# Moving statistics, sums and skip products in a selective-scan kernel: where x's statistics run, where a late sum stands, and which skip products go together

## Chip, cores and metric

The kernel runs on one core of a Trainium2 chip. The metric is the device time of one execution in microseconds; before the change the median of 3 runs is 20936.09 us (20930.49 to 20946.7). All data are 32-bit floats.

## The reference

The input is x of shape (8, 384, 64, 64). Two layers follow each other, each as x + f(groupnorm(x)) with 32 groups. The first is attention over channels, the second a selective scan in four directions:

```python
x = x + L0(gn(x))                          # 1x1 convs, 3x3 depthwise convs, channel attention, projection
xs = cross_scan(gn(x))                     # k = 0 rows, 1 columns, 2 rows reversed, 3 columns reversed
dts, Bs, Cs = split(einsum('bkdl,kcd->bkcl', xs, x_proj_weight), (12, 16, 16))
dt = softplus(einsum('bkrl,kdr->bkdl', dts, dt_projs_weight) + dt_bias)
h = h * exp(dt * A) + dt * u * B           # along l, for each of 16 states n; u = xs
y = sum over n of h * C  +  Ds * u
x = x + gelu(layernorm(cross_merge(y)))
```

A has 4 x 384 x 16 entries, the sequence length is 4096.

## The kernel before

The outer loop goes over 8 images. For each, `channel_attention` runs first, then `selective_scan`. `load_x(b + 1)` fetches the next image near the end of the scan stage into the same three buffers of x, which come free one by one as their last reader, `weigh` of step 31, has run (periods 2, 4 and 6 of step 30). `x_stats` (line 154) takes statistics of the next image in 24 blocks of 128 x 512 on VectorE. The group norm at the start of the next attention stage needs all of them.

The scan stage is written as a hand-made software pipeline. A step s is one direction k and one chunk of 512 positions: 32 steps, 8 for each k. A step has 8 periods p, each of which handles two of the 16 states (a pair). `period(g)` with g = 8 s + p issues, in an order written by hand:

- on VectorE six scans of pair g (`step(0)` to `step(5)`, line 565: two states times three blocks of 128 channels);
- on ScalarE the decays exp(dt A) for scans two ahead (`next_decay(i)` makes the decay for scan i + 2, line 544; two PSUM buffers, so it waits until scan i has freed its own);
- on GpSimd the two products w B of pair g + 1 (`drive`, line 553), sometimes `weigh` for the next step;
- on TensorE, for pair o = g - 1, eight turns q (`turned(q)`, line 587: three transposes of h into one of two PSUM banks), each followed by `apply(q)`, which multiplies by C into `hc` on ScalarE (line 599) or, for the q in `on_dve`, on VectorE (line 601); then sums over the states of the pair into `py` (`add_up`, lines 622 and 628). The output of a step has 512 positions by 384 channels in four blocks `lb`; blocks 0 to 2 are summed in the period after the pair (`added(0..2)`), block 3 one period later (`add_up(o - 1, NJ)`), since its last apply (q = 7) runs only at the start of that period;
- on TensorE also the projections of step s + 2 (`projected(i)`, twelve pieces i over periods 2 to 7, line 451). For k = 1 and 3 these read x with a stride of 64 elements.

For k = 0 the skip connection sum(Ds) * x is added by twelve extra products per step (line 614, inside `add_up`, ahead of the sum of the same block).

Period 1 is the burst: it makes the step size of step s + 1 and adds the finished step s - 1 into `ys` (`take`).

Almost everything is wrapped in `pin`, which is `tc.keep_in_program_order`: the instruction stays behind the one written before it on its engine. What is not pinned is placed by the framework's scheduler. The statistics are not pinned, nor are the DMAs, which all go through SyncE's queue. The statistics are written after the last period: ten before the last `take`, fourteen after it.

What sets the order of the work around the change, in the period for p other than 1:

```python
turned(0); step(0); apply_c(o - 1, 7); turned(1)
if p >= 3: projected(2 * p - 4)
add_up(o - 1, NJ); next_decay(0); step(1); apply(0); turned(2)
next_decay(1); step(2); drive(g + 1, 1); apply(1); turned(3)
added(0); apply(2); turned(4); next_decay(2); step(3); apply(3); turned(5); added(1)
next_decay(3); step(4); apply(4); turned(6); apply(5); turned(7); added(2)
if p == 2: projected(0)
if p >= 2: projected(2 * p - 3)
next_decay(4); step(5); apply(6); next_decay(5)
```

Of the kernel before, what the change touches and what calls it, by code (L numbers as in the profile page):

```python
# [17 lines left out]
NJ = C // P  # L18
H = W = 64
L = H * W  # L20
CH = 512
NCH = L // CH
# [9 lines left out]
NP = N // 2  # L32
HP = P // 2
NQ = CH // HP
PX = 4

FT = 256
JUNK = 512
# [36 lines left out]
def tile_channel_attention_then_selective_scan(ctx: ExitStack, tc: tile.TileContext, a: dict):  # L75
    nc = tc.nc
# [66 lines left out]
    def load_x(b):  # L143

        xs = []
        for j in range(NJ):
            t = big.tile([P, L], F32, tag="x", bufs=NJ, name=f"x{b}_{j}")
            for h in range(2):
                nc.sync.dma_start(t[:, bass.ts(h, L // 2)], x_d[b, j, :, bass.ts(h, L // 2)])
            xs.append(t)  # L150
        stats = big.tile([P, NJ, NCH, nc.vector.BN_STATS_DIM], F32, tag="st0", name=f"st0{b}")
        return xs, stats

    def x_stats(x, stats, blocks):

        for j, c in blocks:
            nc.vector.bn_stats(stats[:, j, c, :], x[j][:, bass.ts(c, CH)])

    def channel_attention(b, x, stats, before):

# [217 lines left out]
    def selective_scan(b, x1, stats1):  # L378
# [10 lines left out]
        with ExitStack() as st:  # L389
# [18 lines left out]
            with tc.tile_pool(name=f"sn{b}", bufs=1) as np_:  # L408
# [4 lines left out]
                for c in range(NCH):  # L413
                    for j in range(NJ):
                        s = x1[j][:, bass.ts(c, CH)]
# [176 lines left out]
            def apply_c(g, q, eng):  # L592
                s, p = divmod(g, NP)
                if q % 2 == 0:
                    hcs[g, q // 2] = work.tile([P, 2, C], F32, tag="hc", bufs=6, name=f"hc{b}_{g}_{q}")
                out, src = hcs[g, q // 2][:, q % 2, :], pts.pop(q)[:, :C]
                scale = cts[s][:, p * NQ + q : p * NQ + q + 1]
                if eng is nc.scalar:
                    pin(eng.activation(out, src, AF.Copy, scale=scale))  # L599
                else:  # L600
                    pin(eng.tensor_scalar_mul(out, src, scale))  # L601

            def add_up(g, lb):

                s, p = divmod(g, NP)
                if p == 0 and lb == 0:
                    pys[s] = ps_y.tile([P, NJ, CH], F32, tag="py", name=f"py{b}_{s}")
                hc, py = hcs.pop((g, lb)), pys[s]
                k, c = steps[s][:2]

                if k == 0 and p >= 2 and p % 2 == lb % 2:
                    j = p // 2 - 1
                    o = py[:, lb, bass.ts(j, P)] if lb < NJ else py[:, j, C:]
                    pin(nc.tensor.matmul(
                        o, lhsT=x1[j][:, c * CH + lb * P : c * CH + (lb + 1) * P],
                        rhs=skip[:, j, :], start=False, stop=False,
                    ))

                flags = dict(start=p == 0 and lb < NJ, stop=p == NP - 1 and lb == NJ)
                if lb < NJ:  # L620
                    for f in range(2):
                        pin(nc.tensor.matmul(  # L622
                            py[f * HP : (f + 1) * HP, lb, :C], lhsT=pair, rhs=hc[:, f, :], **flags
                        ))
                else:
                    for j in range(NJ):
                        for f in range(2):
                            pin(nc.tensor.matmul(  # L628
                                py[f * HP : (f + 1) * HP, j, C:], lhsT=pair,
                                rhs=hc[:, f, bass.ts(j, P)], **flags,  # L630
                            ))
# [61 lines left out]
            def period(g):  # L693

                o, s, p = g - 1, g // NP, g % NP  # L700
                last = g == S * NP
                burst = p == 1 and s + 1 < S
                on_dve = {3, 4, 5} if burst else {0: {2}, 2: {4}}.get(p, set())
                taken = s - 1 if p == 1 and s > 0 else None

                def step(i):
                    if not last:
                        scan(g, *divmod(i, NJ))

                def next_decay(i, home=None):  # L710
                    if not last:
                        decay(g, *divmod(i + 2, NJ), home)

                def apply(q):
                    if o >= 0:
                        apply_c(o, q, nc.vector if q in on_dve else nc.scalar)

                def turned(q):
                    if o >= 0:
                        turn(o, q)  # L720

                def added(lb):
                    if o >= 0:
                        add_up(o, lb)

                def projected(i):
                    if s + 2 < S:
                        project(s + 2, i)

                def take_all():  # L730
                    if taken is not None:
                        for i in range(NJ):
                            take(taken, i)

                if not last:
                    h2s[g] = work.tile([P, NJ, CH, 2], F32, tag="h", bufs=3, name=f"h{b}_{g}")
                    if p == 2:
                        sum_of(s)
                if o >= 0:
                    keep_last(o)  # L740
                fetch(g + 3)
                drive(g + 1, 0)
                if p == 3 and s + 1 < S:
                    mingle_c(s + 1)
                if p in (2, 4, 6) and s + 1 < S:
                    weigh(s + 1, p // 2 - 1)
                turned(0)
                step(0)
                if o >= 1:
                    apply_c(o - 1, NQ - 1, nc.scalar)  # L750
                turned(1)
                if p >= 3:
                    projected(2 * p - 4)
                if o >= 1:
                    add_up(o - 1, NJ)
                next_decay(0)
                step(1)
                apply(0)
                turned(2)
                next_decay(1)  # L760
                step(2)
                drive(g + 1, 1)
                apply(1)
                if burst:
                    pds = step_matmuls(s + 1)
                    apply(2)
                    next_decay(2)
                    next_decay(3, work)
                    step_size(s + 1, pds)
                    step(3)  # L770
                    step(4)
                    take_all()
                    step(5)
                    turned(3)
                    turned(4)
                    added(0)
                    apply(3)
                    turned(5)
                    apply(4)
                    turned(6)  # L780
                    added(1)
                    next_decay(4)
                    next_decay(5)
                    apply(5)
                    turned(7)
                    added(2)
                    apply(6)
                    return
                turned(3)
                if p == 1:  # L790
                    take_all()
                added(0)
                if p == 0 and 0 < s < S - 1:
                    lay_out(s + 1)
                apply(2)
                turned(4)
                next_decay(2)
                step(3)
                apply(3)
                turned(5)  # L800
                added(1)
                next_decay(3)
                step(4)
                apply(4)
                turned(6)
                apply(5)
                turned(7)
                added(2)
                if p == 2:
                    projected(0)  # L810
                if p >= 2:
                    projected(2 * p - 3)
                if p == 0 and s < S:
                    turn_c(s)
                next_decay(4)
                step(5)
                apply(6)
                next_decay(5)
                if p == 0 and s < S:
                    keep_c(s)  # L820

            x_next = None
            for g in range(S * NP + 1):
                period(g)
                if g == (S - 1) * NP + 1 and b + 1 < B:
                    x_next = load_x(b + 1)
            apply_c(S * NP - 1, NQ - 1, nc.scalar)
            add_up(S * NP - 1, NJ)
            blocks = [(j, c) for j in range(NJ) for c in range(NCH)]
            if x_next:  # L830
                x_stats(*x_next, blocks[:10])
            for i in range(NJ):
                take(S - 1, i)
            if x_next:
                x_stats(*x_next, blocks[10:])
        return y_d, x_next

    def token_norm(b, keep, work, y_d):
# [110 lines left out]
```

## Time and profile before

| | us |
|---|---|
| median of 3 runs | 20936.09 |
| profiled execution | 20922.88 |
| its span | 20921.1 |
| scan stage of one image, first scan to end of the last (images 0 to 6 / 7) | 2109.0 to 2111.5 / 2091.2 |
| from the start of the last period of an image to the first scan of the next | 499.8 to 504.0 |

The scan stages are about four fifths of the span. Their structure is seen best in the length of each period, taken from the trace as the distance between the first scans of two periods (median over images and steps, us):

| steps | direction now / two steps ahead | p 0 | 1 | 2 | 3 | 4 | 5 | 6 | 7 |
|---|---|---|---|---|---|---|---|---|---|
| 0 to 5 | rows, with skip / rows | 7.71 | 11.00 | 8.30 | 7.58 | 7.60 | 8.27 | 7.55 | 8.26 |
| 6 and 7 | rows, with skip / columns | 7.73 | 10.99 | 8.31 | 7.95 | 7.89 | 8.46 | 7.89 | 8.46 |
| 8 to 13 | columns / columns | 7.71 | 10.83 | 8.30 | 7.95 | 7.75 | 7.75 | 7.75 | 7.76 |
| 14 and 15 | columns / rows | 7.71 | 10.83 | 8.30 | 7.43 | 7.55 | 7.55 | 7.55 | 7.55 |
| 16 to 21 | rows / rows | 7.71 | 10.83 | 8.24 | 7.44 | 7.49 | 7.49 | 7.49 | 7.49 |
| 22 to 29 | rows, columns / columns | 7.71 | 10.83 | 8.24 | 7.89 | 7.70 | 7.69 | 7.69 | 7.69 |
| 30 | columns / none | 7.71 | 10.83 | 9.40 | 10.01 | 11.17 | 10.01 | 11.20 | 10.01 |

The rows differ in the direction of the step itself, in whether the projections of two steps ahead are contiguous (rows) or strided (columns), and in whether the step carries skip products. In a row of the profile the columns are the line, the engine, the operation, output and inputs with shapes, and the count; after the bar stand the busy time, the mean duration in ns, and the idle time of the engine just ahead of them with what ended it. A timeline line gives start and length in us of a run of like instructions, and in brackets the idle time ahead of it.

### The profile page before, as it was taken

The numbers are of one execution on the slowest core, as the hardware profiler recorded it, in microseconds if no ns is written. First come the engines' busy times: TensorE is split into PE (matmuls) and PEld (weight loads), VectorE is DVE, ScalarE is ACT, GpSimd is POOL, SyncE is SP. The second block draws the span as 40 slices with busy tenths as digits, with TensorE's granted clock in tenths as the row PEclk, the third lists the DMA queues.
The fourth block names the chain that finished last, engine by engine and source line by source line (L and its number), as shares of the span: only waits on it lengthen the run. The fifth ranks groups of instructions, "written<-read, shape, count | busy, mean of one in ns | idle before, by whom it ended". The sixth has DMA issues, their size and how long they took to land. (4 is left out here: it accounts for less than half of the span.)

```text
span 20921.1 us, 319325 instructions
## 1 busy us (share of the span) xinstructions
PE 19277.1 (92%) x118256; PEld 10697.2 (51%) x118256; DVE 19312.5 (92%) x17310; ACT 18022.9 (86%) x32267; POOL 15437.3 (74%) x6918
## 2 busy tenths in 40 slices
PE   7999989999899998999989999899998999989998
PEld 4555445555455554555445555455544555445554
DVE  8999989999899988999889998899988999889998
ACT  3999949999599985999859998599985999859998
POOL 0999809998199981999719997199971999729997
PEclk8999989999899998999989999899998999989999
DMA  1222322223223232222322223223232232322223
GB/s 41 78 91 93 95 75 81 91 92 96 73 81 91 92 99 70 81 91 92 102 69 81 91 92 102 70 79 91 93 99 71 81 92 92 97 71 82 91 91 116
DMA packets 953163, 1807.95 MB, mean 86 GB/s; under 512 B 125904, under 2 KB 646352, under 8 KB 945456
## 3 DMA queue, kind: packets, MB, share of 16 engines
q1 hardware_dynamic: 950736, 1787.40, 27.0%
q8 instruction: 932, 15.27, 0.3%
q14 instruction: 631, 5.17, 0.1%
q10 hardware_dynamic: 864, 0.12, 0.0%
HBM read 1468.39 MB, written 318.77 MB: 85 GB/s over the span
## 5 line engine op out<-in xcount | busy, mean ns | idle before, releaser
L553 POOL TENSOR_TENSOR db<-w,B 128x1536 f32<-128x1536 f32 x4088 | 14134.1, 3464 | 639.9 <-DVE h L565 283.9
L565 DVE TENSOR_TENSOR_SCAN h<-da,ca,db 128x512 f32<-128x512 f32 x10752 | 13085.7, 1268 | 627.2 <-ACT da L544 316.6
L599 ACT ACTIVATE hc<-pt,ct 128x384 f32<-128x384 f32 x15128 | 8517.5, 579 | 452.1 <-PE pt L587 353.0
L544 ACT ACTIVATE da<-dt,neg_a 128x512 f32<-128x512 f32 x12288 | 8508.7, 696 | 183.3 <-DVE h L565 148.2
L587 PE MATMUL pt<-ident,h 128*128 128x128 f32 x49152 | 8097.9, 288 | 582.9 <-ACT hc L599 412.3
L587 PEld LDWEIGHTS pt<-ident,h 128*128 128x128 f32 x49152 | 5150.5, 141 | 5243.1 <-ACT hc L599 2648.5
L622 PE MATMUL py<-hc,pair 128*64 128x384 f32 x24576 | 5347.7, 514 | 9.2 <-DVE ys L673 9.2
L402 POOL MEMSET wdt<- 128x1536 f32 x8 | 11.0, 1378 | 3614.3 <-DMA x1d<-x 3614.3
L628 PE MATMUL py<-hc,pair 128*64 128x128 f32 x24576 | 2114.2, 281 | 0.0
L565 DVE TENSOR_TENSOR_SCAN h<-da,db 128x512 f32<-128x512 f32 x1536 | 1814.0, 1232 | 160.6 <-ACT da L544 98.9
L622 PEld LDWEIGHTS py<-hc,pair 128*64 128x64 f32 x24576 | 1218.5, 135 | 1020.3 <-issue 950.9
L628 PEld LDWEIGHTS py<-hc,pair 128*64 128x64 f32 x24576 | 1568.5, 137 | 208.9 <-issue 130.4
L451 PE MATMUL px<-x,wx 128*44 128x128 f32 x6144 | 1482.4, 339 | 35.3 <-ACT x L417 29.1
L451 PEld LDWEIGHTS px<-x,wx 128*44 128x44 f32 x6144 | 649.1, 122 | 816.7 <-issue 750.9
L528 POOL TENSOR_TENSOR w<-x,dt 128x512 f32<-128x512 f32 x744 | 1056.0, 1419 | 0.0
L579 POOL COPY ca<-h 128x6 f32<-128x6 f32 x1792 | 339.3, 189 | 943.7 <-DVE h L565 940.4
L510 PE MATMUL pd<-xd,wdt 128*128 128x512 f32 x1536 | 781.5, 618 | 73.0 <-ACT hc L599 60.6
L601 DVE TENSOR_SCALAR hc<-pt,ct 128x384 f32<-128x384 f32 x1256 | 736.2, 603 | 54.8 <-PE pt L587 25.4
L349 PE MATMUL pp<-v,mT 128*128 128x512 f32 x1152 | 556.1, 637 | 121.8 <-DVE v L240 57.3
L520 ACT ACTIVATE dt<-pd,dt_bias 128x512 f32<-128x512 f32 x768 | 474.6, 685 | 21.3 <-PE pd L510 17.7
L510 PEld LDWEIGHTS pd<-xd,wdt 128*128 128x128 f32 x1536 | 274.6, 192 | 387.0 <-issue 187.1
L349 PEld LDWEIGHTS pp<-v,mT 128*128 128x128 f32 x1152 | 229.5, 205 | 402.0 <-issue 314.4
(315 smaller groups left out, 11723.8 us busy)
## 6 DMA issues: line engine op xcount, KB each, us to landing
B<-bcd SPq DMA_DIRECT2D x2048, 512.0 KB
yd<-ys SPq DMA_DIRECT2D x128, 576.0 KB
ys<-yd SPq DMA_DIRECT2D x256, 288.0 KB
yd<-ys SPq DMA_DIRECT2D x256, 288.0 KB
x<-in_x SPq DMA_DIRECT2D x48, 1024.0 KB
x1d<-x SPq DMA_DIRECT2D x192, 256.0 KB
fy<-yd SPq DMA_DIRECT2D x128, 384.0 KB
fin<-yd SPq DMA_DIRECT2D x112, 384.0 KB
```

The lines of the kernel that those rows point to most:

```text
L349: nc.tensor.matmul(pc, lhsT=mT[:, j, bass.ts(m, P)], rhs=v[:, j, bass.ts(c, CH)], start=j == 0, stop=j == NJ - 1,)
L451: pin(nc.tensor.matmul(split(pxs[s][:XR, :])[:, part, :], lhsT=wx[:, j, k, :], rhs=view(x1[j], k, c)[:, part, :], start=i == 0, stop=i == ...
L510: pin(nc.tensor.matmul(pds[j], lhsT=wdt[:, k, bass.ts(j, P)], rhs=xds[s], start=True, stop=True))
L528: pin(eng.tensor_mul(split(ws[s][:, j, :]), view(x1[j], k, c), split(dts[s][:, j, :])))
L544: pin(nc.scalar.activation(t, dts[s][:, j, :], AF.Exp, scale=neg_a[:, j, k, n : n + 1]))
L553: pin(eng.tensor_mul(t, ws[g // NP], bts[g][:, v : v + 1, :].broadcast_to([P, NJ, CH])))
L565: pin(nc.vector.tensor_tensor_scan(h, da, db, 0.0 if start else carries[s - 1][:, j, n : n + 1], ALU.mult, ALU.add,))
L587: pin(nc.tensor.transpose(t[:, bass.ts(j, P)], h2s[g][:, j, bass.ts(q, HP), :].rearrange("p l v -> p (l v)"), ident))
L599: pin(eng.activation(out, src, AF.Copy, scale=scale))
L601: pin(eng.tensor_scalar_mul(out, src, scale))
L622: pin(nc.tensor.matmul(py[f * HP : (f + 1) * HP, lb, :C], lhsT=pair, rhs=hc[:, f, :], **flags))
L628: pin(nc.tensor.matmul(py[f * HP : (f + 1) * HP, j, C:], lhsT=pair, rhs=hc[:, f, bass.ts(j, P)], **flags,))
```

## The change

Four edits, all to the order of the scan stage:

1. The statistics of the next image are pinned. They are taken one by one after each of periods 4 to 7 of step 31, four before the last (257th) period call, one after it, six before the last apply, and nine after the last sums.
2. In a period p >= 2 for which step s + 2 exists and is strided (`odd`), the sum of block 3 stands behind turn 2 instead of behind turn 1, and projection 0 is issued in period 2 before turn 2 instead of at its end.
3. In period 2, VectorE does apply 2 instead of apply 4.
4. The skip products are spread by a table, two to each pair of states from pair 2 to 7, where they were two to each by parity; each block still gets all three channel groups.

```diff
@@ -33,6 +33,8 @@
+SKIPS = {2: (0, 1), 3: (2, 3), 4: (0, 3), 5: (1, 3), 6: (0, 2), 7: (1, 2)}
@@ -154,7 +156,9 @@
     def x_stats(x, stats, blocks):
 
         for j, c in blocks:
-            nc.vector.bn_stats(stats[:, j, c, :], x[j][:, bass.ts(c, CH)])
+            tc.keep_in_program_order(
+                nc.vector.bn_stats(stats[:, j, c, :], x[j][:, bass.ts(c, CH)])
+            )
@@ -608,8 +612,8 @@
-                if k == 0 and p >= 2 and p % 2 == lb % 2:
-                    j = p // 2 - 1
+                if k == 0 and lb in SKIPS.get(p, ()):
+                    j = sum(lb in SKIPS[i] for i in SKIPS if i < p)
@@ -700,7 +704,7 @@
-                on_dve = {3, 4, 5} if burst else {0: {2}, 2: {4}}.get(p, set())
+                on_dve = {3, 4, 5} if burst else {0: {2}, 2: {2}}.get(p, set())
@@ -749,14 +753,18 @@
                 turned(1)
-                if p >= 3:
+
+                odd = p >= 2 and s + 2 < S and steps[s + 2][0] % 2 == 1
+                if p >= 3 or odd:
                     projected(2 * p - 4)
-                if o >= 1:
+                if o >= 1 and not odd:
                     add_up(o - 1, NJ)
                 next_decay(0)
                 step(1)
                 apply(0)
                 turned(2)
+                if o >= 1 and odd:
+                    add_up(o - 1, NJ)
@@ -806,7 +814,7 @@
-                if p == 2:
+                if p == 2 and not odd:
                     projected(0)
@@ -820,19 +828,27 @@
             x_next = None
+            blocks = [(j, c) for j in range(NJ) for c in range(NCH)]
+
+            def stats_next(n):
+                if x_next:
+                    x_stats(*x_next, blocks[:n])
+                    del blocks[:n]
+
             for g in range(S * NP + 1):
+                if g == S * NP:
+                    stats_next(4)
                 period(g)
                 if g == (S - 1) * NP + 1 and b + 1 < B:
                     x_next = load_x(b + 1)
+                if g >= (S - 1) * NP + 4:
+                    stats_next(1)
+            stats_next(6)
             apply_c(S * NP - 1, NQ - 1, nc.scalar)
             add_up(S * NP - 1, NJ)
-            blocks = [(j, c) for j in range(NJ) for c in range(NCH)]
-            if x_next:
-                x_stats(*x_next, blocks[:10])
             for i in range(NJ):
                 take(S - 1, i)
-            if x_next:
-                x_stats(*x_next, blocks[10:])
+            stats_next(len(blocks))
         return y_d, x_next
```

## The prediction

> **What bounds the kernel now.** The page comes first: which engines are full, and which rows they are full of.
>
> ```profile
> PE 19277.1 (92%) x118256; PEld 10697.2 (51%) x118256; DVE 19312.5 (92%) x17310; ACT 18022.9 (86%) x32267; POOL 15437.3 (74%) x6918
> L565 DVE TENSOR_TENSOR_SCAN h<-da,ca,db 128x512 f32<-128x512 f32 x10752 | 13085.7, 1268 | 627.2 <-ACT da L544 316.6
> ```
>
> Four engines are nearly full, so shares decide nothing. The second view is the start of each period's first scan, from the trace (table above). A plain period with contiguous projections lasts 7.49 us, with strided ones 7.69 to 7.75. The timeline shows why. First a contiguous period (step 18, period 5, from 6920.60), then a strided one (step 29, period 4, from 7628.13).
>
> ```profile
> 6922.62 0.31 PE L451 MATMUL px<-x,wx 128*44 128x128 f32 x1
> 6923.62 0.55 PE L587 MATMUL pt<-ident,h 128*128 128x128 f32 x3
> 6923.72 1.07 ACT L599 ACTIVATE hc<-pt,ct 128x384 f32<-128x384 f32 x2
> ...
> 7630.15 0.40 PE L451 MATMUL px<-x,wx 128*44 128x128 f32 x1
> 7631.36 1.06 PE L587 MATMUL pt<-ident,h 128*128 128x128 f32 x6
> 7631.26 1.27 ACT L599 ACTIVATE hc<-pt,ct 128x384 f32<-128x384 f32 x2
> 7633.14 2.46 DVE L565 TENSOR_TENSOR_SCAN h<-da,ca,db 128x512 f32<-128x512 f32 x2 [0.20 <-ACT da L544]
> ```
>
> Seen from the period's start, turn 2 begins at 3.02 in the first and at 3.23 in the second, since projection and late sum stand before it on PE. ACT's apply(1) and apply(2) take 1.07 back to back in the first and 1.27 in the second: apply(2) waits for turn 2. Behind it on ACT stands the decay for scan 4, and scan 4 stalls 0.20. The cycle that sets the period is: scans 0 and 1 (2.46), then on ACT decay, two applies, decay, apply, decay, two applies, decay, at 0.61 per decay and 0.47 per apply (start to start in the trace), the last running its full 0.70 and 0.09 to the next scan 0: 7.49. PE delays move the period only through turn 2.
>
> Third, the same timeline where skip products stand before turn 2 (step 3, period 5, from 5934.74), and in period 2 of step 18 (from 6897.43):
>
> ```profile
> 5937.25 0.49 PE L614 MATMUL py<-skip,x 128*128 128x128 f32 x2
> 5939.12 0.58 ACT L599 ACTIVATE hc<-pt,ct 128x384 f32<-128x384 f32 x1 [0.59 <-PE pt L587]
> 5940.31 2.46 DVE L565 TENSOR_TENSOR_SCAN h<-da,ca,db 128x512 f32<-128x512 f32 x2 [0.77 <-ACT da L544]
> ...
> 6901.00 1.24 PE L587 MATMUL pt<-ident,h 128*128 128x128 f32 x6
> 6902.78 1.28 DVE L565 TENSOR_TENSOR_SCAN h<-da,ca,db 128x512 f32<-128x512 f32 x1 [0.26 <-ACT da L544]
> 6903.98 0.59 DVE L601 TENSOR_SCALAR hc<-pt,ct 128x384 f32<-128x384 f32 x1
> ```
>
> A skip product for block 3 stands before turn 2 and stalls scan 4 by 0.77. In period 2 turn 2 is itself late (3.57 to 4.11) and the DVE apply comes after scan 4.
>
> Fourth, DVE in step 30 and at the end of the scan stage, then the windows for step 30 from period 2 on, in the last image (which has no statistics to take) and in the one before:
>
> ```profile
> 7706.83 1.29 DVE L157 BATCH_NORM_STATS2 st<-x 128x6 f32<-128x512 f32 x2 [1.64 <-DMA x<-in_x]
> 7710.39 0.67 DVE L157 BATCH_NORM_STATS2 st<-x 128x6 f32<-128x512 f32 x1
> 7729.14 1.29 DVE L157 BATCH_NORM_STATS2 st<-x 128x6 f32<-128x512 f32 x2 [3.29 <-DMA x<-in_x]
> 7805.86 0.62 DVE L601 TENSOR_SCALAR hc<-pt,ct 128x384 f32<-128x384 f32 x1 [3.18 <-PE pt L587]
> 7811.13 1.88 DVE L673 TENSOR_TENSOR ys<-ys,py 128x512 f32<-128x512 f32 x3 [4.65 <-PE py L628]
> 7818.84 0.83 DVE L114 BATCH_NORM_AGGREGATE mv<-st 128x2 f32<-128x48 f32 x3 [5.83 <-DMA yd<-ys]
> ...
> 20701.80:20747.30 45.50, 42.15 (x297) 22.86 (x296) 44.02 (x39) 44.83 (x84) 44.07 (x21) 1.00 0.31 89
> 18097.80:18159.50 61.70, 49.66 (x294) 25.94 (x291) 57.05 (x60) 47.35 (x84) 45.60 (x23) 0.86 0.57 173
> ```
>
> The statistics, though written last, run between the scans of step 30 and wait there for x to land, while DVE idles 3.18, 4.65 and 5.83 us in the tail.
>
> **What the Trainium skill says.** "Perfetto Trace Analysis", Tensor Engine Instruction: ACT, DVE and GpSimd are strict queues, and PE's end times are modelled. The trace agrees with the first (whatever follows a late apply(2) is late), so I use PE starts alone. The same page, Optimization Strategy: the same gap repeating can mean too few buffers; here turn 2 needs the bank that apply(0) frees, and the gap is 0.20 in each strided period. "SBUF — State Buffer", Door 1, on 16-byte lines: reads that leave a line each time pay. The two matmuls of a projection start 0.14 apart contiguous and 0.22 strided, which agrees. No page prices the statistics; the trace does.
>
> **Statistics.** Step 30 costs 64.05 us in the last image and 80.7 on average in the seven others, step 31 up to its last period 54.17 against 54.87: 17.35 us per image, 121 in seven. New places: three blocks stand between periods of step 31. One adds 0.59 to DVE's queue (0.67 less overlap), where scan 0 waits 0.23 for its decay anyway: +0.35, 1 us per image. Five stand between the last scan and the tail's apply: 5 x 0.59 = 3.0 in 3.18 idle. Seven stand before the sums: 4.1 in 4.65, and nothing may be late there, since the stores and the whole next stage follow. The last nine, 5.3, lie in 5.83, and the aggregation after them leads to a 6.59 wait for DMA and PE. x has landed by then (issued behind the last weighings of step 30). If a cover fails it costs its overlap, under 1 us per image. Net -121 + 7 = **-114**; bounds -95 and -121.
>
> **Late sums in odd steps** (the step two ahead is strided: 6 to 13 and 22 to 29, 16 per image). Nothing is removed. PE's twelve sum matmuls (0.8 us) go behind turn 2; projection 0 goes from period 2's end to before its turn 2. Plain period, PE starts: turn 1 at 1.54, projection 2.02, turn 2 then 2.62 (bound by apply(0), done at 2.57) instead of 3.23. Apply(2) is back at 3.61 and the stall of scan 4 goes. What is late next: the sum runs 3.07 to 3.88, so turn 3 is at 3.88 (3.74), the sum of block 0 at 4.35, turn 4 at 5.15 to 5.70 against apply(4) at 5.77, turn 6 at 6.75 to 7.30 against apply(6) at 7.31. It fits by hundredths. PE's whole period, start to start, sums to 7.48 to 7.53 (turns 3.4, sums of blocks 0 to 2 2.3, late sum 0.8, projections 1.0), as long as the cycle. I take 7.52 for 7.69 (rows 22 to 29) and 7.75 (8 to 13), with 7.46 and 7.65 as ends. Period 3 now begins with projections 0 and 1 still to run on PE; 0 has gone, so it becomes like the others: 7.89 and 7.95 to 7.52. Period 2: turn 2 moves from 3.57 to 3.26 although the projection comes before it; with the apply on DVE (below) -0.23. Per step: 0.23 + 0.37 + 4 x 0.17 = 1.28 (64 steps), 0.23 + 0.43 + 4 x 0.23 = 1.58 (48 steps). Steps 6 and 7 also carry skips and are PE's own length; I take 1.0 (16 steps). 82 + 76 + 16 = **-174**; bounds -85 and -195.
>
> **Apply 2 instead of 4 on DVE in period 2.** In even steps DVE would run it right after scan 2, at 3.67, but turn 2 ends at 4.11. So DVE waits 0.5, and scans 3, 4 and 5 queue behind it: scan 3 at 4.67, scan 5 at 7.05, where it is now (7.05). ACT gets apply(4) back, so the decay for the next scan 0 ends at 8.24 instead of 7.61, and the period ends at 8.3 and the next one loses a lead of 0.05. +0.1 in 128 steps: **+13**; bounds -25 and +26.
>
> **Skip products.** Twelve per step as before. Blocks 0 to 2 of pair p run in period p+1, block 3 in p+2. Counts by period 3,4,5,6,7,0,1 go from 2,1,3,1,3,1,1 to 2,1,2,2,3,2,0. But only block 3 stands before turn 2, and it stands there in periods 5, 6, 7 instead of 5, 7, 1. Worked by PE starts at 0.34 to 0.42 each in the contiguous steps 0 to 5: period 4 +0.17 (pair 2's block 1 makes the last applies late), 5 -0.1, 6 +0.55 (turn 2 from 3.02 to 3.57), 7 -0.05, 1 -0.13. Sum +0.48 in 48 steps: **+23**; bounds -29, if the even count is what matters, and +40.
>
> **Sum.** -114 - 174 + 13 + 23 = -252. The profiled execution took 20922.88 (span 20921.1), 13 below the median 20936.09: 20671 against that one, 20684 beside the median, which I give.
>
> **Rivals.** (A) As worked, 20684: 0.55. (B) PE becomes the bound of odd periods, since its sum of 7.5 leaves no room for its waits: 7.62 instead of 7.52. Odd gain 85, statistics 105, period 2 +20, skips +35: 20801. For it: PE is busy for all of 23.09 us in three strided periods. Against: the gaps before turns 3 and 5 now are waits for ACT. 0.17. (C) All ends good: 195 + 121 + 25 + 15 = 356: 20580. For it: period 0 has its apply at 2 and lasts 7.71. Against: turn 2 is at 2.83 there. 0.14. (D) Slower: the late sum, now before turn 3, delays turns 4 and 6 beyond apply(4), whose delay reaches the next scan 0. With 114 from the statistics and 36 given back elsewhere it decides from +0.12 per strided period (78 over 128 steps of five periods), thus 7.82, PE at 7.8. At 7.9 in all five: +0.2 x 640 = 128, so 20986. For it: turn 4 has 0.07 of room. Against: no PE work is added. 0.10. (E) The pins or the late order change little on the chip, or the sides cancel: 20936: 0.04.
>
> **Numbers.** Range 20585 to 20810: from C to B. A measurement of this kernel can tell about 0.2% from no change. Faster 0.86 (A, B, C), same 0.04, slower 0.10.
>
> **What would show it.** Strided periods near 7.5 with no wait at scan 4; turn 2 before the row of the late sum; no statistics in step 30, 64 us there, and none of the tail's waits longer; period 6 of steps 0 to 5 at about 8.1. Wrong if strided periods stay above 7.65, or if the sums of the tail start later than 8.5 us after the last scan.

## The result, and the profile after

| us | before | after |
|---|---|---|
| median (4 runs each, taken together) | 20937.25 (20930.49 to 20946.7) | 20748.94 (20747.59 to 20753.39) |
| span of the profiled execution | 20921.1 | 20746.3 |

The ratio is 0.991 with a 95% interval of 0.9894 to 0.9926: 188 us less, where 252 were forecast. The two profiled executions stand 174.8 apart. In their traces the eight scan stages together lose 180 us (first scan to end of the last), the first of them starts 5.3 later, and the attention stages between them differ by up to 3 us in either direction.

The first view is again the page of the changed kernel: busy time by engine, and the row of the scans (after the bar: busy time, mean ns, idle time ahead and its main cause).

```profile
PE 19205.9 (93%) x118256; PEld 10578.6 (51%) x118256; DVE 19321.9 (93%) x17310; ACT 17951.9 (87%) x32267; POOL 15441.2 (74%) x6918
...
L569 DVE TENSOR_TENSOR_SCAN h<-da,ca,db 128x512 f32<-128x512 f32 x10752 | 13058.6, 1267 | 500.2 <-issue 204.3
```

No work went: the counts are those of before and the busy times differ by about 1% at most. The scans' idle time ahead fell from 627.2 to 500.2 us, and a late decay is no longer its main cause. That is part of the gain. What the statistics give is not in this row, since VectorE's waits there stood ahead of the statistics' own instructions.

The lengths of the periods show where it came from (distance of first scans, median in us, before → after). Steps 14 to 21 share a row, from period 2 on with the differences alone; where it has two, the first is for steps 14 and 15 and the second for 16 to 21.

| steps | p 0 | 1 | 2 | 3 | 4 | 5 | 6 | 7 | total us |
|---|---|---|---|---|---|---|---|---|---|
| 0 to 5, skips | 7.71→7.72 | 11.00→11.14 | 8.30→8.34 | 7.58→7.60 | 7.60→7.82 | 8.27→8.12 | 7.55→8.12 | 8.26→8.26 | +40 |
| 6 and 7, skips and strided | 7.73→7.79 | 10.99→11.11 | 8.31→8.24 | 7.95→7.81 | 7.89→7.83 | 8.46→8.20 | 7.89→7.82 | 8.46→8.27 | -10 |
| 8 to 13, strided | 7.71→7.72 | 10.83→10.84 | 8.30→8.24 | 7.95→7.59 | 7.75→7.60 | 7.75→7.60 | 7.75→7.60 | 7.76→7.60 | -47 |
| 22 to 29, strided | 7.71→7.72 | 10.83→10.84 | 8.24→8.18 | 7.89→7.53 | 7.70→7.54 | 7.69→7.54 | 7.69→7.54 | 7.69→7.54 | -64 |
| 14 to 21, contiguous | 7.71→7.72 | 10.83→10.84 | +0.03, +0.10 | +0.11, +0.05 | +0.01 | +0.01 | +0.01 | +0.01 | +13 |
| 30 | 7.71→7.72 | 10.83→10.84 | 9.40→8.34 | 10.01→7.46 | 11.17→7.46 | 10.01→7.46 | 11.20→7.46 | 10.01→7.46 | -115 |

Step 31 adds 1.6. The timeline of the changed kernel shows a strided period (step 29, period 4, scans from 7577.30), with start, length, engine and the number of like instructions in a run:

```profile
7577.30 7.25 DVE L569 TENSOR_TENSOR_SCAN h<-da,ca,db 128x512 f32<-128x512 f32 x6 [0.29 <-POOL ca L583]
...
7579.42 0.61 PE L455 MATMUL px<-x,wx 128*44 128x128 f32 x2
...
7579.97 0.55 PE L591 MATMUL pt<-ident,h 128*128 128x128 f32 x3
7580.42 1.06 ACT L603 ACTIVATE hc<-pt,ct 128x384 f32<-128x384 f32 x2
...
7580.45 0.88 PE L632 MATMUL py<-hc,pair 128*64 128x128 f32 x12
...
7581.25 0.55 PE L591 MATMUL pt<-ident,h 128*128 128x128 f32 x3
...
7582.53 0.87 PE L591 MATMUL pt<-ident,h 128*128 128x128 f32 x6
...
7583.11 1.05 ACT L603 ACTIVATE hc<-pt,ct 128x384 f32<-128x384 f32 x2
...
7584.05 0.69 ACT L548 ACTIVATE da<-dt,neg_a 128x512 f32<-128x512 f32 x1
...
7584.13 0.87 PE L591 MATMUL pt<-ident,h 128*128 128x128 f32 x6
...
7584.71 0.58 ACT L603 ACTIVATE hc<-pt,ct 128x384 f32<-128x384 f32 x1
7584.84 1.28 DVE L569 TENSOR_TENSOR_SCAN h<-da,ca,db 128x512 f32<-128x512 f32 x1 [0.29 <-issue]
```

Turn 2 (7579.97) starts at 2.67 of the period, now ahead of the late sum (L632), and ScalarE's applies 1 and 2 run back to back in 1.06. The six scans are one run without a gap: scan 4 no longer waits. The period is 7584.84 - 7577.30 = 7.54.

VectorE in step 31 and behind it, in the same image as before:

```profile
7710.69 0.67 DVE L160 BATCH_NORM_STATS2 st<-x 128x6 f32<-128x512 f32 x1
...
7733.83 3.04 DVE L160 BATCH_NORM_STATS2 st<-x 128x6 f32<-128x512 f32 x5
7737.09 0.62 DVE L605 TENSOR_SCALAR hc<-pt,ct 128x384 f32<-128x384 f32 x1 [0.22 <-PE pt L591]
7737.63 4.24 DVE L160 BATCH_NORM_STATS2 st<-x 128x6 f32<-128x512 f32 x7
7742.37 1.88 DVE L677 TENSOR_TENSOR ys<-ys,py 128x512 f32<-128x512 f32 x3 [0.50 <-PE py L632]
7744.17 5.43 DVE L160 BATCH_NORM_STATS2 st<-x 128x6 f32<-128x512 f32 x9
7750.07 0.83 DVE L116 BATCH_NORM_AGGREGATE mv<-st 128x2 f32<-128x48 f32 x3 [0.48 <-DVE st L160]
```

Five, seven and nine blocks fill the three gaps of the tail. What VectorE still idles there is 0.22, 0.50 and 0.48, where it was 3.18, 4.65 and 5.83. Nothing behind is late for it: the tail's first sum starts 8.45 after the end of the last scan, in every image of both kernels. Step 30, with no block in it, takes 64.2 in the last image, which has no statistics to take, and in all others but one, which takes 64.6. The windows of the changed kernel, one whole step 30 of that image and of the last (from, to, length, busy time of PE, PEld, DVE, ACT, POOL; then the granted clock, the DMA engines' busy share and GB/s):

```profile
17925.62:17990.19 64.57, 59.74 (x399) 31.76 (x397) 62.35 (x57) 63.15 (x115) 60.83 (x29) 1.00 0.58 190
20507.34:20571.55 64.21, 59.66 (x399) 31.74 (x397) 62.35 (x57) 62.97 (x115) 60.49 (x29) 1.00 0.31 93
```

### The profile page after: what moved, and what is told of

Its sections match the earlier page's. It is cut to its first block, busy times and chain, and to the rows that moved or that the text cites. A ratio compares the mean times of both kernels' runs of the same rounds, so it can differ in the third digit from the quotient of the medians.

```text
span 20746.3 us, 319602 instructions
## 1 busy us (share of the span) xinstructions
PE 19205.9 (93%) x118256; PEld 10578.6 (51%) x118256; DVE 19321.9 (93%) x17310; ACT 17951.9 (87%) x32267; POOL 15441.2 (74%) x6918
## 5 line engine op out<-in xcount | busy, mean ns | idle before, releaser
L569 DVE TENSOR_TENSOR_SCAN h<-da,ca,db 128x512 f32<-128x512 f32 x10752 | 13058.6, 1267 | 500.2 <-issue 204.3
L591 PE MATMUL pt<-ident,h 128*128 128x128 f32 x49152 | 7976.9, 287 | 457.5 <-ACT hc L603 305.0
L632 PE MATMUL py<-hc,pair 128*64 128x128 f32 x24576 | 1871.6, 281 | 0.0
L626 PEld LDWEIGHTS py<-hc,pair 128*64 128x64 f32 x24576 | 1216.6, 135 | 1014.6 <-issue 945.3
L632 PEld LDWEIGHTS py<-hc,pair 128*64 128x64 f32 x24576 | 1377.2, 136 | 267.2 <-issue 240.2
```

What stands on the lines that cost most here:

```text
L569: pin(nc.vector.tensor_tensor_scan(h, da, db, 0.0 if start else carries[s - 1][:, j, n : n + 1], ALU.mult, ALU.add,))
L591: pin(nc.tensor.transpose(t[:, bass.ts(j, P)], h2s[g][:, j, bass.ts(q, HP), :].rearrange("p l v -> p (l v)"), ident))
L626: pin(nc.tensor.matmul(py[f * HP : (f + 1) * HP, lb, :C], lhsT=pair, rhs=hc[:, f, :], **flags))
L632: pin(nc.tensor.matmul(py[f * HP : (f + 1) * HP, j, C:], lhsT=pair, rhs=hc[:, f, bass.ts(j, P)], **flags,))
```

## The experiments

The theory: the parts of the sum act where the prediction put them, and the 64 us that are missing are a chain in the strided periods and TensorE time of the skip products. The rivals: TensorE's own length is the bound of the strided periods (B of the prediction), or the parts disturb each other. Each result is the median with its ratio to the kernel before of the same chip; differences in us are to those runs of before unless another kernel is named. Such other comparisons are between chips on which the kernel before lies within 2 us (20935.5 to 20937.3).

### Each part alone

**Statistics alone.** The edit is the diff's part on `x_stats` and `stats_next`, and nothing else.

> Only the statistics are moved; sums, skips and the apply of period 2 are as before. By the period table of the changed kernel step 30 falls from 80.3 to about 64.1 us and step 31 grows by 1 in each of seven images, and the tail hides the rest: 113 us less than before, about 20823. Rival: part of the 175 us gained there came from the other edits sharing the step, or the tail gives some back; then the gain is under 90.

Measured: 20807.57, ratio 0.9944 (0.9929 to 0.9959), -116. Period 3 to 7 of step 30 last 7.43 to 7.46, and the steps before it are unchanged. The part is worth what was forecast.

**Late sums alone**, the edit on `odd`:

```diff
-                if p >= 3:
+
+                odd = p >= 2 and s + 2 < S and steps[s + 2][0] % 2 == 1
+                if p >= 3 or odd:
                     projected(2 * p - 4)
-                if o >= 1:
+                if o >= 1 and not odd:
                     add_up(o - 1, NJ)
...
                 turned(2)
+                if o >= 1 and odd:
+                    add_up(o - 1, NJ)
...
-                if p == 2:
+                if p == 2 and not odd:
                     projected(0)
```

> Only the late sum and projection 0 are moved. If turn 2 is what strided projections delay, strided periods fall to 7.54 (steps 22 to 29) and 7.60 (steps 8 to 13), period 3 to the same, contiguous steps do not move, and the run is 115 to 130 us below before, about 20815. Period 2 of odd steps should fall by under 0.1 with the old apply too, if the late sum ahead of turn 3 is what holds it; by 0.2 or more if the apply on VectorE holds it.

Measured: 20797.51, ratio 0.9939 (0.9925 to 0.9954), -126. Strided periods 4 to 7 last 7.54 in steps 22 to 29 and 7.60 in 8 to 13; period 2 lasts 8.18 in both (0.06 and 0.12 less); contiguous steps are unchanged. So this part alone holds the larger share of the shortfall, and it is no disturbance by the other three.

**Apply 2 in period 2 alone:**

```diff
-                on_dve = {3, 4, 5} if burst else {0: {2}, 2: {4}}.get(p, set())
+                on_dve = {3, 4, 5} if burst else {0: {2}, 2: {2}}.get(p, set())
```

> Only period 2 has apply 2 on VectorE in place of apply 4. VectorE then waits for turn 2 about 0.4 us in every step: period 2 longer by 0.05 to 0.1 and period 3 by up to 0.1, in 256 steps some 15 to 35 us slower than before. Rival: it frees ScalarE where it is late, and the kernel gets faster by as much.

Measured: 20958.62, ratio 1.0016 (1.0009 to 1.0023), +35; by the trace 15.5 in the contiguous steps and 19.5 in the strided ones. In the changed kernel the strided part of it is not there: with the late sums, periods 2 and 3 of steps 8 to 13 sum to 8.24 + 7.59 = 15.83 with this edit, and to 8.18 + 7.64 = 15.82 without it.

**Skip products alone**, the edit on `SKIPS` (the table itself is that of the change):

```diff
-                if k == 0 and p >= 2 and p % 2 == lb % 2:
-                    j = p // 2 - 1
+                if k == 0 and lb in SKIPS.get(p, ()):
+                    j = sum(lb in SKIPS[i] for i in SKIPS if i < p)
```

> Only the table of skip products is new. If block 3's product ahead of turn 2 and a skip ahead of the transpose of C are what cost, periods 1, 4 and 6 of steps 0 to 5 grow by 0.14, 0.2 and 0.57 and period 5 falls by 0.14: 35 to 45 us slower than before. Rival: the number of products per period is what counts; then the more even table is faster.

Measured: 20974.6, ratio 1.0024 (1.0015 to 1.0033), +51, somewhat more than expected; the trace has 39 in steps 0 to 5 and 9 in steps 6 and 7. In steps 0 to 5 periods 1, 4, 5, 6 move by +0.13, +0.22, -0.14, +0.57. Period 6 in the timeline of this kernel (step 3, from 5962.61):

```profile
5964.98 0.49 PE L616 MATMUL py<-skip,x 128*128 128x128 f32 x2
...
5966.20 0.87 PE L589 MATMUL pt<-ident,h 128*128 128x128 f32 x6
...
5966.85 0.58 ACT L601 ACTIVATE hc<-pt,ct 128x384 f32<-128x384 f32 x1 [0.56 <-PE pt L589]
...
5968.04 2.46 DVE L567 TENSOR_TENSOR_SCAN h<-da,ca,db 128x512 f32<-128x512 f32 x2 [0.63 <-ACT da L546]
```

A product for block 3 (5964.98) and the late sum stand ahead of turn 2, which starts at 3.59. Apply(2) waits 0.56, and the decay queued behind it on ScalarE stalls scan 4 by 0.63. Period 1 went the other way than the prediction had it. The timeline of the changed kernel there, from the end of step 3's period 0 (period 1 begins at 5859.99):

```profile
5859.82 0.39 PE L618 MATMUL py<-skip,x 128*128 128x128 f32 x2
...
5860.94 0.27 PE L484 MATMUL pct<-ident,cy 64*128 64x64 f32 x1
...
5861.24 0.21 ACT L492 COPY ct<-pct 128x64 f32<-128x64 f32 x1 [0.28 <-PE pct L484]
```

A second product in period 0 makes the transpose of C for the new step start at 0.95 of period 1. Before, in the same place:

```profile
5900.98 0.27 PE L480 MATMUL pct<-ident,cy 64*128 64x64 f32 x1
...
5901.28 0.21 ACT L488 COPY ct<-pct 128x64 f32<-128x64 f32 x1
```

There, with the period from 5900.25, it starts at 0.73 and ScalarE's copy has no wait. Now the copy waits 0.28 on ScalarE, and the first apply and all behind it with it. A product fewer in period 1 itself doesn't make up for that.

The four parts alone sum to -116 - 126 + 35 + 51 = -156, the whole change to -188: apply 2 costs less beside the late sums.

**Statistics and late sums, without the other two.** The edit is that of the first two runs together.

> The statistics and the late sums of the change, with the old table of skips and apply 4 in period 2. If the parts add as they did alone (-116 and -126), 20923 - 242 = 20681, which is some 60 below the changed kernel. Rival: new table and late sum need each other (steps 6 and 7 carry both); then it gains under 215.

Measured: 20693.36, ratio 0.9883 (0.9869 to 0.9898), -242, which is -116 - 126 more closely than such medians can tell. So these two add up, and apply 2 with the skips costs the changed kernel 56 us, of which the trace puts 40 in steps 0 to 5, and 10 in steps 14 to 21.

### What the skips cost, and where they should stand

**The late sum behind turn 2 also where block 3 has a product** (the changed kernel, rows too):

```diff
-                if o >= 1 and not odd:
+                late = odd or (o >= 1 and steps[(o - 1) // NP][0] == 0 and NJ in SKIPS.get((o - 1) % NP, ()))
+                if o >= 1 and not late:
                     add_up(o - 1, NJ)
...
-                if o >= 1 and odd:
+                if o >= 1 and late:
```

> The changed kernel, and block 3's sum goes behind turn 2 in contiguous steps too wherever it has a skip product ahead of it (pairs 3, 4 and 5). If the skip costs through turn 2, periods 5, 6 and 7 of steps 0 to 5 fall from 8.12, 8.12 and 8.27 to about 8.0, 7.85 and 8.1, 20 to 30 us in all. If it is the amount of work on TensorE, they do not move.

Measured: 20729.83, ratio 0.9901 (0.9886 to 0.9916), 19 below the changed kernel. Period 5 falls from 8.12 to 8.00 and 6 from 8.12 to 7.82; period 7, with three products, stays at 8.27, where 8.1 had been expected. By the trace steps 0 to 5 give 15 of the 19. A product ahead of turn 2 costs more than the same one behind it.

**Products in fixed places, whichever block they belong to.** A product may be added to `py` ahead of any sum of its step once the first pair has begun that block. Here twelve of them stand ahead of the sums of blocks 0 and 2 (0 and 1 for the last pair), in the kernel with statistics and late sums alone:

```diff
+SKIPS = [(l, j) for l in range(NQ // 2) for j in range(NJ)]
...
-                if k == 0 and p >= 2 and p % 2 == lb % 2:
-                    j = p // 2 - 1
+                if k == 0 and p >= 2 and lb in ((0, 1) if p == NP - 1 else (0, 2)):
+                    l, j = SKIPS[2 * (p - 2) + (lb > 0)]
...
```

The product then goes to block `l` of `py` instead of `lb`.

> As the run with statistics and late sums alone, with the twelve skip products issued two per pair ahead of the sums of blocks 0 and 2 (0 and 1 for the last pair), whichever block they belong to: none ahead of turn 2, none ahead of the transpose of C. Periods 3 to 7 of steps 0 to 5 should be 7.6 to 7.75 and period 1 10.85: some 40 to 50 us below that run, about 20635. If TensorE's amount of work binds, no gain.

Measured: 20638.38, ratio 0.9856 (0.9842 to 0.9871), 55 below the kernel it starts from. Periods 3 to 7 of steps 0 to 5 last 7.58 and four times 7.62. Its timeline (step 3, period 5, from 5854.97):

```profile
5858.05 1.23 PE L591 MATMUL pt<-ident,h 128*128 128x128 f32 x6
...
5859.11 0.39 PE L618 MATMUL py<-skip,x 128*128 128x128 f32 x2
```

The six transposes are turns 2 and 3. Turn 2 starts at 3.08, ahead of this product and of the second one at 5862.53. They still cost something, but 0.06 and not 0.6: 7.62 against 7.56 in steps 14 and 15, whose scans also run forward (7.50 is the period of the reversed ones). Steps 6 and 7, which have strided projections as well, gained nothing. Period 1 is 11.15, where 10.85 had been expected and the kernel it starts from has 11.01: a miss that this run and that of the skips alone explain together, since both have two products in period 0.

**One product moved from the last pair to pair 1:**

```diff
-                if k == 0 and p >= 2 and lb in ((0, 1) if p == NP - 1 else (0, 2)):
-                    l, j = SKIPS[2 * (p - 2) + (lb > 0)]
+                if k == 0 and p >= 1 and lb in {1: (2,), NP - 1: (1,)}.get(p, (0, 2)):
+                    l, j = SKIPS[0 if p == 1 else 2 * p - 3 + (lb == 2)]
```

> As the run with new skip places, with one product moved from the last pair to pair 1, so that period 0 has one in place of two and period 2 one at its end. If TensorE's lateness in period 0 reaches period 1 through the transpose of C and its copy on ScalarE, period 1 of steps 0 to 7 falls from 11.15 to about 11.0 and the run is 5 to 15 us below that one, about 20628. If period 2 or 3 grows as much, no gain.

Measured: 20633.79, ratio 0.9856 (0.9842 to 0.9871), 5 less than the kernel above, which such medians hardly tell apart; the trace does. Period 1 falls from 11.15 to 10.93, so the second product of period 0 was what held it. That is 12 us; some 4 come back as periods 3 of steps 0, 6 and 7 grow by 0.14 to 0.15. Of the rest 3 us are scatter: in every kernel period 2 of an image's first step is 1.5 longer in some images than in others, in five of them there and in seven here.

### What bounds a strided period

**The projection behind turn 2 as well** (the changed kernel). If TensorE's work alone counted, its order would not.

```diff
-                if p >= 3 or odd:
+                if p >= 3 and not odd:
                     projected(2 * p - 4)
...
                 turned(2)
+                if odd:
+                    projected(2 * p - 4)
```

> The changed kernel, but in strided steps the projection too goes behind turn 2, ahead of the late sum. If the projection is what fills TensorE's wait for apply 0, TensorE now idles about 0.5 before turn 2 and strided periods grow from 7.54 to 7.8 or more: over 150 us slower than the changed kernel. If turn 2 only has to be early, nothing is lost, or a little gained, since projection and sum overlap again.

Measured: 21052.88, ratio 1.0054 (1.0037 to 1.0071), 304 above the changed kernel, with the same instructions. Strided periods last 7.94 and 8.00. Its timeline (step 29, period 5, from 7698.72):

```profile
7700.77 0.57 ACT L603 ACTIVATE hc<-pt,ct 128x384 f32<-128x384 f32 x1
...
7701.39 0.55 PE L591 MATMUL pt<-ident,h 128*128 128x128 f32 x3 [0.48 <-ACT hc L603]
...
7703.07 0.55 PE L591 MATMUL pt<-ident,h 128*128 128x128 f32 x3
...
7703.66 0.58 ACT L603 ACTIVATE hc<-pt,ct 128x384 f32<-128x384 f32 x1 [0.18 <-PE pt L591]
...
7706.66 1.28 DVE L569 TENSOR_TENSOR_SCAN h<-da,ca,db 128x512 f32<-128x512 f32 x1 [0.52 <-ACT da L548]
```

TensorE has nothing left ahead of turn 2, and idles 0.48 there until apply(0) has freed the bank: turn 2 starts at 2.67, no earlier than in the changed kernel. Projection and sum then come behind it, so turn 3 is at 4.35 and its apply waits 0.18. Turn 3 is 0.40 later than in the changed kernel (3.96), and the period is longer by the same 0.40. The projection ahead of turn 2 fills a wait that is there anyway.

**A third of the projections left out**, the changed kernel in strided periods 3 to 6:

```diff
-                if p >= 2:
+                if p >= 2 and not (odd and 3 <= p <= 6):
                     projected(2 * p - 3)
```

> The changed kernel without four of the twelve projection pieces of each strided step (the one at the end of periods 3 to 6), so that the projections are incomplete: 0.5 to 0.6 us less for TensorE in these periods. If TensorE's own length sets the strided period at 7.54 and 7.60, the next three periods (4 to 6) fall to what contiguous ones take, 7.49 to 7.50 and 7.55, and steps 6 and 7 to 7.6 to 7.7. If it is the cycle of VectorE and ScalarE, they stay.

Measured, one run: 20744.17, and strided periods stay at 7.54 and 7.60. Its timeline (step 29, period 5, from 7582.47):

```profile
7584.06 0.55 PE L591 MATMUL pt<-ident,h 128*128 128x128 f32 x3 [0.15 <-ACT hc L603]
...
7584.54 0.61 PE L455 MATMUL px<-x,wx 128*44 128x128 f32 x2
...
7585.14 0.55 PE L591 MATMUL pt<-ident,h 128*128 128x128 f32 x3
...
7587.70 0.87 PE L591 MATMUL pt<-ident,h 128*128 128x128 f32 x6
...
7590.01 1.28 DVE L569 TENSOR_TENSOR_SCAN h<-da,ca,db 128x512 f32<-128x512 f32 x1 [0.29 <-issue]
```

What TensorE saves becomes idle time, 0.15 of it ahead of turn 1. The remaining projection starts at 2.07, 0.05 earlier than in the changed kernel, but turn 2 is again at 2.67 and turn 4 at 5.23. Steps 6 and 7, which carry skip products too, lose 0.15 in period 5 alone, where 7.6 to 7.7 had been given for the rival. So the rival that TensorE's sum is the bound of the plain strided periods falls. GpSimd is no rival either: it is busy nearly without a gap in periods 3 to 7, but so it is in step 30, with the same products, and there a period lasts 7.46. Turn 2 waits for apply(0), which ends at 2.62, and from there a chain runs on: late sum, turn 3, sum of block 0, turn 4, and with it turn 6. Apply(4) and apply(6) wait for these two turns, and ScalarE's row leads on to the next apply(0). In the medians of steps 22 to 29 of the changed kernel apply(4) starts 0.69 and apply(6) 0.66 behind the start of the decay ahead of it; in step 30, where neither waits, it is 0.61. Worked out from these, the chain by way of turn 6 is 0.04 longer than that by apply(4), so turn 6 is its last link.

**The late sum in two pieces.** To shorten that chain without removing work, the first 4 of the late sum's 12 matmuls stand ahead of turn 2, the other 8 behind it, in strided periods 3 to 7 of the best kernel above (that with a product at pair 1):

```diff
-            def add_up(g, lb):
+            def add_up(g, lb, js=range(NJ)):
...
+                if odd and p > 2:
+                    add_up(o - 1, NJ, (0,))
...
                 turned(2)
                 if o >= 1 and odd:
-                    add_up(o - 1, NJ)
+                    add_up(o - 1, NJ, (1, 2) if p > 2 else range(NJ))
```

> As the run with one product moved to pair 1, and in strided periods 3 to 7 the late sum is split: its first four of twelve matmuls stay ahead of turn 2, where TensorE waits for apply 0 anyway, the other eight go behind. If the late sum between turns 2 and 3 is what keeps strided periods at 7.54 and 7.60 (turn 4, then apply 4), they fall to 7.49 to 7.50 and 7.50 to 7.56: 25 to 35 us below that run, about 20605. If turn 2 becomes late again, they grow towards 7.6 to 7.7.

Measured: 20614.38 (20612.32 to 20618.06), ratio 0.9847 (0.9834 to 0.9861), 19 below the kernel it starts from (17 by the traces), less than the 25 to 35 expected. Steps 8 to 13 fall from 7.60 to 7.54 or 7.55, steps 22 to 29 only from 7.54 to 7.53. Its timeline (step 10, period 5, from 6310.17):

```profile
6312.68 0.40 PE L632 MATMUL py<-hc,pair 128*64 128x128 f32 x2
...
6313.01 0.55 PE L591 MATMUL pt<-ident,h 128*128 128x128 f32 x3
...
6313.48 0.66 PE L632 MATMUL py<-hc,pair 128*64 128x128 f32 x8
...
6315.34 0.88 PE L591 MATMUL pt<-ident,h 128*128 128x128 f32 x6
...
6315.99 1.05 ACT L603 ACTIVATE hc<-pt,ct 128x384 f32<-128x384 f32 x2
...
6317.71 1.28 DVE L569 TENSOR_TENSOR_SCAN h<-da,ca,db 128x512 f32<-128x512 f32 x1 [0.30 <-issue]
```

Turn 4 starts at 5.17 instead of 5.23, and the period shortens by the same 0.06: the chain was the bound in these steps. Here the chain is open: turn 2 starts at 2.84 (2.89 in steps 22 to 29), 0.2 after apply(0) has ended, so it no longer waits for it, and the trace shows TensorE without a gap from one turn 0 to the next, for 7.53 to 7.54. TensorE's own length in this order is thus the likely bound now, 0.01 under the chain of steps 22 to 29. It is not shown: no run took work from TensorE in this kernel, and the missing gap alone proves nothing, since the changed kernel has none either, and there the run above did take work away and gained nothing.

This is also the best version: 135 us below the changed kernel and 321 below the one before.

### Whether the statistics need their places

All 24 blocks behind the last period, ahead of the last sums (the changed kernel, with nothing in the loop and `stats_next(24)` for `stats_next(6)`):

```diff
-                if g == S * NP:
-                    stats_next(4)
                 period(g)
...
-                if g >= (S - 1) * NP + 4:
-                    stats_next(1)
-            stats_next(6)
+            stats_next(24)
```

> The changed kernel with all 24 blocks of statistics between the last scan and the last sums. They take 24 x 0.59 = 14.2 us; the waits there cover 3.2 and 4.65, so the sums and all behind them are 6.3 later per image, and 1.1 is saved in step 31: about 36 us slower than the changed kernel. Rival: the wait of the next stage for its weights and averages hides the sums too, and the time does not change.

Measured: 20805.74, ratio 0.994 (0.9923 to 0.9956), 57 above the changed kernel, where 36 had been expected. VectorE in the tail of this kernel:

```profile
7750.46 0.62 DVE L605 TENSOR_SCALAR hc<-pt,ct 128x384 f32<-128x384 f32 x1 [3.18 <-PE pt L591]
7750.99 14.33 DVE L160 BATCH_NORM_STATS2 st<-x 128x6 f32<-128x512 f32 x24
...
7772.93 0.83 DVE L116 BATCH_NORM_AGGREGATE mv<-st 128x2 f32<-128x48 f32 x3 [5.83 <-DMA yd<-ys]
```

The blocks are queued behind the tail's apply on VectorE, so the 3.18 ahead of it covers none of them, and the 5.83 ahead of the aggregation is open again. Only the gap of 4.65 is used: 14.3 - 4.65 = 9.6 per image, and the trace has 9.4. The expectation had counted the 3.18 as cover as well. An idle wait covers only work that is queued ahead of the waiting instruction, not work near it.

## Why the prediction was right, and where it was off

**What bounds the kernel:** held in the main. Contiguous steps stay at 7.49 to 7.50 (7.55 to 7.56 in steps 14 and 15), and in the strided ones the wait at scan 4 went. But the cycle of scans and ScalarE's row is 7.46 and not 7.49: that is what step 30 takes, which has no projections. In contiguous steps turn 2 is still a little late. Apply(2) starts there 0.49 behind apply(1), and 0.55 in steps 14 and 15, against 0.46 in step 30.

**Statistics, -114:** right, -116 alone. Step 30 lasts 64.2 us as in the last image, the three blocks between periods of step 31 cost 0.25 to 0.27 each in most images (0.35 forecast), and the tail's gaps cover theirs.

**Late sums, -174:** the sign, the place and period 3 (7.53 and 7.59) were right; the size was -126, and this is the term that fails. It does so at two points.

- "It fits by hundredths": it doesn't quite. That room is the distance from the modelled end of a turn to its apply: 5.70 to 5.77 for turn 4, 7.30 to 7.31 for turn 6. Measured, an apply that waits for its turn alone starts 0.58 after the start of the turn in steps whose scans are reversed, and 0.64 in forward ones (medians, at turn 2 of the kernel before as at turns 4 and 6 of the changed one). From the prediction's own turn 6 at 6.75, apply(6) can then start at 7.33 and 7.39, not at 7.31: it is short by 0.02 and 0.08. In the changed kernel apply(6) is late, and the first decay in the next period starts at 0.35 and not at 0.29. So apply(0) ends at 2.62 and turn 2 starts at 2.67 instead of 2.62; turn 3 is at 3.96 (3.88 forecast) and turn 4 at 5.23 (5.15). Apply(4) then starts at 5.81 in steps 22 to 29 and at 5.88 in 8 to 13, instead of 5.77. Every strided period is 0.02 and 0.08 longer than the 7.52 I took. Over 64 and 48 steps of five periods, and in steps 6 and 7, that is some 28 us.
- Period 2 was given -0.23 and moved by -0.06 to -0.12, about 16 us. I followed turn 2 (3.30, where 3.26 was forecast) and scan 5 and took the period as ended there, but its end is the decay for the next scan 0. The timeline of the changed kernel (step 29, period 2, from 7561.59):

```profile
7565.37 0.88 PE L632 MATMUL py<-hc,pair 128*64 128x128 f32 x12
...
7566.17 0.55 PE L591 MATMUL pt<-ident,h 128*128 128x128 f32 x3
...
7566.76 0.58 ACT L603 ACTIVATE hc<-pt,ct 128x384 f32<-128x384 f32 x1 [0.38 <-PE pt L591]
...
7568.97 0.69 ACT L548 ACTIVATE da<-dt,neg_a 128x512 f32<-128x512 f32 x1
```

The late sum now stands ahead of turn 3 (4.58), apply(3) waits 0.38 for it on ScalarE, and the decay for the next scan 0 ends at 8.07, which makes the period 8.18. The prediction had asked what is late next in the plain period, and not in this one.

**Apply 2, +13:** right in the contiguous steps, 15.5 alone. VectorE waits 0.40 for it (0.5 forecast), and period 2 goes from 8.24 to 8.34. That it costs strided steps as much again without the late sums, and nothing with them, the sum could leave out.

**Skip products, +23:** the second term that was mis-sized; with the steps that I hadn't counted it costs 45 to 50. Periods 4, 5, 6 and 7 were given +0.17, -0.1, +0.55, -0.05 and moved by +0.22, -0.14, +0.57, 0. But period 1 was given -0.13 and moved by +0.14: I subtracted a product from period 1's own queue and left out that the one added in period 0 stands ahead of the transpose of C, for which ScalarE's copy and every apply behind it wait. Steps 6 and 7 weren't counted at all (+9 alone). The five terms given add up to +0.44 per step and not +0.48, thus +21; nor does C's 15 for the skips match their bound of 29. Neither slip bears on the result.

**The sum.** -242 instead of -288 for the first two, +56 instead of +36 for the others: -186, against 188 between the medians. The result lies between A (20684) and B (20801), in number a little nearer to B. The two misses don't cancel: the late sums gave less and the skips cost more, both on the slow side, and the result is in the range because that reaches as far as B. In mechanism it is neither A nor B: B's bound, TensorE's own length, may lie at 7.53 and not at 7.62, just under the chain that decides. That chain is the one that D named, the late sum ahead of turns 3, 4 and 6. It acts by 0.02 to 0.08 per period, where D needed 0.3. The Trainium skill ("Perfetto Trace Analysis", Tensor Engine Instruction) has it that the profiler estimates when a TensorE instruction ends. The prediction named this, said that it would use starts alone, and still measured its last room from such ends. These traces agree with the page: ScalarE starts 0.58 or 0.64 after the start of a turn whose end is put at 0.55 in both cases.

## What to carry to other kernels

When an instruction is moved out of one wait, follow every instruction that is now behind it to the end of the period, in each kind of period by itself, and find there which engine's last instruction releases the next one; room of hundredths, taken from modelled ends, is no room. A wait in a queue that runs in order covers only work queued ahead of it: filling gaps means placing pieces, as the 24 blocks at the tail and the skip products show. And what must be added to a full queue goes right behind the instruction others wait for, whichever piece of the result it belongs to.

## What the runs showed that was not expected

- ScalarE's start behind the same turn differs with the direction of the scans. In the changed kernel turn 4 starts at 5.23 both in step 29 (reversed) and in step 10 (forward), yet apply(4) starts at 5.81 in the first, and here at 5.88:

```profile
6364.90 0.87 PE L591 MATMUL pt<-ident,h 128*128 128x128 f32 x6
...
6365.55 1.05 ACT L603 ACTIVATE hc<-pt,ct 128x384 f32<-128x384 f32 x2
```

  From start to start that is 0.65 against 0.58 (medians 0.64 and 0.58), and it is all of the difference between the strided periods of 7.60 and 7.54. Turn 2 and apply(2) show the same two figures in contiguous steps, 0.64 in steps 14 and 15 and 0.58 in 16 to 21, where the periods are 7.56 and 7.50. The cause wasn't tried.
- A strided projection with the late sum right behind it takes 1.21 us from its start to the next turn (medians: 3.15 to 4.36 in the run with both behind turn 2). Apart they take 0.52 (at the end of the period in the changed kernel, where the turn behind it waits for nothing) and 0.81, or 1.33. In the first the timeline shows matmuls of the two interleaved, so some of the slow reads seem to lie beside the sum's; that reading wasn't tested by itself.
